# A Perceiver block on one core: VectorE and ScalarE in written order in the second cross-attention, and four longer step distances

## The chip, the cores and the metric

One Trainium2 chip, of which the kernel uses one core. The metric is the device time of one execution in microseconds (us), compared between runs of the kernel before and after the change on the same chip. PE is TensorE, PEld its weight loads, DVE VectorE, ACT ScalarE, POOL GpSimd, SP SyncE (it issues DMAs only).

## What is computed

Two layers over x of 16 x 64 rows of 256 numbers, all in float32. Each layer is a cross-attention to a context of 1024 rows per batch, a self-attention and a feed-forward part, each behind a layernorm and added to x. Cut to its shape:

```python
x = x + _L0_xattn_ref(_layernorm(x), ctx_1024, mask_BxS2_bf0, ...)      # 16 heads of 16
x = x + _L0_attn_ref(_layernorm(x), ...)                                # causal over the 16 batches
x = x + _L0_ffn_ref(_layernorm(x), ...)                                 # 8 experts, top 2
x = x + _L1_xattn_ref(_layernorm(x), ctx_1024, fside_BxS2_0, mask_BxS2_bk0, ...)
x = x + _L1_attn_ref(_layernorm(x), ...)                                # over the 64 rows of a batch
x = x + _L1_ffn_ref(_layernorm(x), ...)                                 # fp4 quantization, gate * up, down

def _L1_xattn_ref(tgt, mem, attn_bias, memory_key_padding_mask, ...):
    q = (tgt @ Wq_w.T + Wq_b).reshape(b, sq, 16, 16)
    kv = (mem @ Wkv_w.T + Wkv_b).reshape(b, sk, 2, 16, 16)
    scores = einsum('bthd,bshd->bhts', q, k * scale) + attn_bias + pad
    return einsum('bhts,bshd->bthd', softmax(scores), v).reshape(b, sq, 256) @ out_w.T + out_b
```

## The kernel before

**Rows and slots.** The 1024 rows lie in eight tiles x[0] to x[7] of 128 rows, so two batches share a tile. A cross-attention walks over 64 slots (batch, half of the heads, half of the keys), b the slowest and the key half the fastest. Four pairs of heads (g = 0 to 3) are worked on at a time; an odd slot holds the second half of the keys of the same heads.

**A slot.** In pass i of the loop, `scores` runs two slots ahead: four score matmuls (L567), each into a bank of PSUM, and four VectorE reductions (L578) that add the mask, write the tile e and keep a minimum. Where slot i + 2 holds a second half, four exponentials on ScalarE (L589) follow, one per e of 128 x 1024. Then slot i itself is turned: four groups k of four transposes (L597), each group into one bank, copied into eT by `evacuate` (L226 on VectorE, L228 on ScalarE; VectorE takes the first two groups of odd slots). At the end of the pass `attend` multiplies slot i - 1 with the values (L611). PSUM has eight banks; the attention's sum `pso` has one, everything else takes turns on the other seven.

**Keys and values.** The second cross-attention finds those of the first nine batches ready in DRAM, made during the first layer's later parts. Those of the other seven are projected in place, two steps per slot (L394 and L409), in slots 32 to 59; their results are evacuated by VectorE in odd slots and by ScalarE in even ones.

**Chains.** Everything that belongs to finished rows is written as generators that run beside the slots. `advance()` resumes every chain once, oldest first, after each group of transposes, so four times per slot; a `yield` is one step of distance, and `bare(n)` is n of them. `end(b)` starts at the end of slot 4b + 4 with `outputs`: copy of the sum (`ot`), reciprocal of the sums (`rec`, L628), turning (L633), scaling (`osb`, L636), and for the second batch of a tile a second turning (L649), `oT`, and the output projection `project_rows` (L322). In the second layer the same chain goes on with `row_attention` (layernorm L258 to L275, projections L1373, rotation L1393, scores L1428, exponential L1446, turning L1452, output L1468 and L1479, projection) and `feed_forward` (layernorm, quantization `fp4` in three steps, two halves of `hidden` L1520 with Silu L1523 and the product L1524, `fp4` of each half, `turn_hidden` L1530, `down` L1545). `queries` makes the queries of the next tile: it adds the two expert outputs that were gathered (`arrive`, L1279), normalizes, turns and projects. One tile takes eight slots, and a chain is longer than that, so that a tile's feed-forward runs beside the next tile's attention.

**What sets the order.** A planner (the tile framework) orders the instructions of each engine at build time, by priority (earlier in the program first) and by when its own timing model takes the inputs as ready. Inside `manual_schedule` the named engines are kept in the order in which the program is written. Before the change this holds for TensorE alone:

```python
            with tc.manual_schedule(engines={mybir.EngineType.PE}):
```

VectorE, ScalarE, GpSimd and the DMA queues are ordered by the planner in both cross-attentions. On the chip each engine runs the order that it was given.

Of the kernel before, what the change touches and what calls it, by code (L numbers as in the profile page):

```python
# [13 lines left out]
AF = mybir.ActivationFunctionType  # L14
# [106 lines left out]
def kernel(ctx: ExitStack, tc: tile.TileContext, a: dict, out: bass.AP):  # L121
    nc = tc.nc
# [127 lines left out]
    def bare(n):  # L250

        for _ in range(n):
            yield
# [77 lines left out]
    def cross_attention(layer, wq, wkv, wo, bq, bk, bv, bo, mask, keep, bias, after, ready, arrive, idle):  # L331
        side = "right" if layer else "left"
        with ExitStack() as st:
# [216 lines left out]
            slots = [(b, dt, hf) for b in range(B) for dt in range(KC) for hf in range(2)]  # L550
            mn, sums, es, eT, po, osb = {}, {}, {}, {}, {}, {}
            NG = 4

            def scores(b, dt, hf):


                if dt == 0 and hf == 0:
                    mn[b] = two.tile([P, 2, NP], F32, name="mn")
                    sums[b] = two.tile([P, NP], F32, name="sums")
                if hf == 0:  # L560
                    for g in range(NG):
                        es[b, dt, g] = wide.tile([P, SK], F32, name="e")
                cols = slice(hf * 512, (hf + 1) * 512)
                sc = [bank() for _ in range(NG)]
                for g in range(NG):
                    r = 32 * g
                    nc.tensor.matmul(  # L567
                        sc[g],
                        qm[b // 2][r : r + 32, dt, b % 2, :, :].rearrange("p j q -> p (j q)"),
                        kT[b][r : r + 32, dt, cols],  # L570
                        start=True,
                        stop=True,
                    )
                for g in range(NG):
                    pr = dt * NG + g
                    e = es[b, dt, g]

                    nc.vector.tensor_tensor_reduce(  # L578
                        out=e[:, cols],
                        in0=sc[g],  # L580
                        in1=negb[b][:, cols],
                        scale=1.0,
                        scalar=3e38 if hf == 0 else mn[b][:, 0, pr : pr + 1],
                        op0=ALU.add,
                        op1=ALU.min,
                        accum_out=mn[b][:, hf, pr : pr + 1],
                    )
                    if hf == 1:
                        nc.scalar.activation(  # L589
                            e, e, AF.Exp, scale=-1.0, bias=mn[b][:, 1, pr : pr + 1], accum_out=sums[b][:, pr : pr + 1]  # L590
                        )

            def transpose_keys(b, dt, k, vector):

# [24 lines left out]
            def outputs(b):  # L619


                n, half = b // 2, b % 2
                ot = two.tile([P, KC, P], F32, name="ot")
                evacuate(ot, po.pop(b), False)
                yield
                yield
                rec = two.tile([P, NP], F32, name="rec")
                nc.vector.reciprocal(rec, sums[b])  # L628
                if half == 0:
                    osb[n] = two.tile([P, NP, 2, HD], F32, name="osb")  # L630
                pq = bank()
                for c in range(KC):
                    nc.tensor.transpose(pq[:, c * P : (c + 1) * P], ot[:, c, :], ident)  # L633
                pov = pq[:, :D].rearrange("p (r j d) -> p r j d", j=2, d=HD)
                for j in range(2):
                    nc.vector.tensor_tensor(  # L636
                        osb[n][half * SQ : (half + 1) * SQ, :, j, :],
                        pov[j * SQ : (j + 1) * SQ, :, j, :],
                        rec[j * SQ : (j + 1) * SQ, :].unsqueeze(2).to_broadcast([SQ, NP, HD]),
                        ALU.mult,  # L640
                    )
                if half == 0:
                    return
                yield
                yield
                pt = bank()
                rows = osb[n].rearrange("p r j d -> p (r j d)")
                for c in range(KC):
                    nc.tensor.transpose(pt[:, c * P : (c + 1) * P], rows[:, c * P : (c + 1) * P], ident)  # L649
                oT = two.tile([P, KC, P], F32, name="oT")  # L650
                for c in range(KC):

                    nc.vector.tensor_scalar(
                        oT[:, c, :], pt[:, c * P : (c + 1) * P], colbias(bv, c), None, ALU.add
                    )
                yield
                yield
                project_rows(n, oT, wo, None if layer else rowbias(bo))
# [20 lines left out]
            def advance():  # L679
                for o in list(chains):  # L680
                    if next(o, o) is o:
                        chains.remove(o)
# [14 lines left out]
            else:  # L697
                load_keys(0)
                load_mask(0)
            with tc.manual_schedule(engines={mybir.EngineType.PE}):  # L700
                arrive(0, two, 0)
                chains.append(queries(0))
                if 0 not in ready:
                    project(0, 0)
                    advance()
                    project(0, 1)
                while chains:
                    advance()
                if not layer:
                    for w, source in soon[:2]:  # L710
                        nc.sync.dma_start(w, source)
                    load(1)
                    for w, source in soon[2:]:
                        nc.sync.dma_start(w, source)
                scores(*slots[0])
                scores(*slots[1])
                if 0 not in ready:
                    for step in range(2, NP):
                        project(0, step)
                for i in range(len(slots) + 1):  # L720

                    vector = i % 2 == 1
                    if i + 2 < len(slots):
                        scores(*slots[i + 2])
                    steps = due.pop(i, [])
                    for part in range(2):
                        for step in [s for s in steps if len(s) == 2][part::2]:
                            project(*step, vector)
                        for step in [s for s in steps if len(s) == 3]:
                            project_seven(*step, part)  # L730
                        if i < len(slots):
                            b, dt, hf = slots[i]
                            for k in (4 * hf + 2 * part, 4 * hf + 2 * part + 1):
                                transpose_keys(b, dt, k, vector and part == 0)
                                advance()
                    if i > 0:
                        b, dt, hf = slots[i - 1]
                        for k in range(4 * hf, 4 * hf + 4):
                            attend(b, dt, k)
                        if dt == KC - 1 and hf == 1:  # L740
                            chains.append(end(b))
                            next(chains[-1])
                    if i % 4 == 0 and i // 4 + 2 < B:
                        load(i // 4 + 2)
                        if seven:
                            sum_context(i // 4 + 2)
                        if i == 4:
                            for w, source in later:
                                nc.sync.dma_start(w, source)
                            later.clear()  # L750
                    if not layer and i == 4 * (B - 1) - 1:
                        for first in load_first:
                            load_ahead(first)
                    if i % 8 == 0 and i // 8 + 1 < NT:
                        arrive(i // 8 + 1, two, 0)
                    if i % 8 == 2 and i // 8 + 1 < NT:
                        chains.append(queries(i // 8 + 1))
                        next(chains[-1])
                while chains:
                    advance()  # L760
                    advance()
                    idle(1)
# [587 lines left out]
    def last_layers(one):  # L1350
# [11 lines left out]
        def row_attention(n, two):  # L1362
# [2 lines left out]
            nc.gpsimd.tensor_tensor(x[n], x[n], rowbias("L1_attn_b_proj"), ALU.add)  # L1365
            yield from bare(4)
            xT = transposed_rows(two, xn)
            yield
            yield
            pm = bank()  # L1370
            for i, (w, dt) in enumerate((w, dt) for w in (wq, wk) for dt in range(KC)):
                for c in range(KC):
# [76 lines left out]
            for dt in range(KC):  # L1449
# [5 lines left out]
                        ident,  # L1455
                    )
                evacuate(eT[:, dt, :, :], pt.rearrange("p (g q) -> p g q", g=NG), False)
            yield
            yield


            po = [bank() for _ in range(2)]
# [38 lines left out]
        def feed_forward(n, two):  # L1501
# [63 lines left out]
            else:  # L1565
# [6 lines left out]
                turn_hidden(0)  # L1572
                yield
                yield from fp4(tiles, h[:, halves[1]], h[:, halves[1]], P, NI - 3 * P, 3 * P)
                yield from bare(2)
                turn_hidden(3)
                yield from bare(3)
                py = bank()[:, :D]
# [109 lines left out]
```

## Time and profile before

| | |
|---|---|
| time, median of 3 runs (lowest to highest) | 1532.1 us (1530.3 to 1533.7) |
| the profiled execution's own time | 1533.16 us |
| its span, first to last instruction | 1531.1 us |
| first layer and what lies before the second cross-attention | 0 to 868 us |
| slots of the second cross-attention | 868 to 1440 us |
| rest of the last two chains | 1440 to 1531 us |
| turns of eight slots without projections in place (slots 9-16, 17-24, 25-32) | 58.9, 74.6, 77.9 us |
| turns with them (33-40, 41-48, 49-56) | 86.5, 85.5, 85.4 us |
| exponentials L589 | 256 x 1139 ns |
| score reductions L578 | 512, of 685 ns (first key half) and 747 ns (second) |
| eT copies | 384 x 587 ns on ScalarE, 128 x 682 ns on VectorE |

A slot is taken here from the start of one group of score matmuls to the start of the next, and numbered by its pass i of the loop. The profile lists for each engine how long it was busy, and for a wait the instruction that ended it. A wait on one of the seven banks shows as a wait on the instruction that emptied the bank, a VectorE reduction or a copy, and not on a producer of data.

### The profile page before, as it was taken

The numbers are of one execution on the slowest core, as the hardware profiler recorded it, in microseconds if no ns is written. First come the engines' busy times: TensorE is split into PE (matmuls) and PEld (weight loads), VectorE is DVE, ScalarE is ACT, GpSimd is POOL, SyncE is SP. The second block draws the span as 40 slices with busy tenths as digits, with TensorE's granted clock in tenths as the row PEclk, the third lists the DMA queues.
The fourth block names the chain that finished last, engine by engine and source line by source line (L and its number), as shares of the span: only waits on it lengthen the run. The fifth ranks groups of instructions, "written<-read, shape, count | busy, mean of one in ns | idle before, by whom it ended". The sixth has DMA issues, their size and how long they took to land.

```text
span 1531.1 us, 33572 instructions
## 1 busy us (share of the span) xinstructions
PE 1393.2 (91%) x13796; PEld 997.1 (65%) x13796; DVE 953.7 (62%) x2573; ACT 759.2 (50%) x1385; POOL 336.2 (22%) x368
## 2 busy tenths in 40 slices
PE   6999999999999898999999789787889999999954
PEld 3677667776776655668888566565656767666732
DVE  3577767777777432365730277786867586767654
ACT  2565666565656531223221476665645555555620
POOL 4344443343332120013300022120201011110000
PEclk9999999999999999999999799898999999999977
DMA  6111101110101022277773332322101111000000
GB/s 231 59 36 40 52 32 33 37 58 33 32 29 56 37 96 71 92 262 230 253 277 120 125 125 98 128 80 77 52 22 35 49 53 49 22 26 1 5 1 7
DMA packets 53556, 119.53 MB, mean 78 GB/s; under 512 B 4908, under 2 KB 25004, under 8 KB 51100
## 3 DMA queue, kind: packets, MB, share of 16 engines
q1 hardware_dynamic: 50732, 112.21, 21.8%
q0 software_dynamic: 1568, 4.26, 1.0%
q8 instruction: 108, 1.77, 0.5%
q10 hardware_dynamic: 1104, 0.93, 0.2%
q14 instruction: 44, 0.36, 0.1%
HBM read 94.32 MB, written 23.07 MB: 77 GB/s over the span
## 4 chain that ended last, share of the span: by engine, by line
PE 72%; DVE 16%; ACT 6%; issue 3%; DMA 2%; POOL 1%; ACTq 0%; DVEq 0%; SPq 0%; POOLq 0%
PE psw L597 11%; PE psw L567 9%; PE pso L611 8%; PE psw L458 6%; PE psw L462 5%; DVE e L578 5%; ACT e L589 4%; PE psw L1227 4%; PE psw L796 4%; PE psw L1247 4%; PE psw L409 3%; PE psw L394 3%; PE psw L783 3%; PE psw L1520 2%; PE psw L1545 2%
## 5 line engine op out<-in xcount | busy, mean ns | idle before, releaser
L589 ACT ACTIVATE e<-e,mn 128x1024 f32<-128x1024 f32 x256 | 291.1, 1139 | 114.5 <-DVE mn L578 113.7
L597 PEld LDWEIGHTS psw<-consts,e 128*128 128x128 f32 x2048 | 240.5, 144 | 104.1 <-issue 62.4
L597 PE MATMUL psw<-consts,e 128*128 128x128 f32 x2048 | 287.3, 280 | 8.3 <-ACT e L589 4.3
L228 ACT COPY eT<-psw 128x512 f32<-128x512 f32 x384 | 209.3, 587 | 156.2 <-PE psw L597 156.2
L578 DVE CUSTOM_DVE_ANT_0 e<-psw,negb,mn 128x512 f32<-128x512 f32 x256 | 179.6, 747 | 138.6 <-PE psw L567 138.6
L578 DVE CUSTOM_DVE_ANT_0 e<-psw,negb 128x512 f32<-128x512 f32 x256 | 163.0, 685 | 67.4 <-PE psw L567 67.4
L567 PE MATMUL psw<-kT,qm 32*128 32x512 f32 x1024 | 170.4, 682 | 8.5 <-DVE mn L578 4.4
L611 PE MATMUL pso<-eT,v 128*32 128x128 f32 x4096 | 146.9, 287 | 0.0
L611 PEld LDWEIGHTS pso<-eT,v 128*32 128x32 f32 x4096 | 110.2, 114 | 27.7 <-issue 26.2
L226 DVE COPY eT<-psw 128x512 f32<-128x512 f32 x128 | 83.0, 682 | 7.5 <-PE psw L597 7.5
L567 PEld LDWEIGHTS psw<-kT,qm 32*128 32x128 f32 x1024 | 52.9, 195 | 42.5 <-issue 22.8
L796 PE MATMUL psw<-w_L_xattn_Wkv_w,actx 128*128 128x256 f32 x288 | 74.2, 411 | 2.2 <-issue 1.4
L359 POOL TENSOR_SCALAR negb<-m 128x1024 f32<-128x1024 uint8 x16 | 16.7, 1045 | 264.4 <-DVE mn L578 214.7
L783 PE MATMUL psw<-actx,w_L_xattn_Wkv_w 128*128 128x512 f32 x144 | 67.4, 608 | 1.3 <-DVE x L769 1.3
L796 PEld LDWEIGHTS psw<-w_L_xattn_Wkv_w,actx 128*128 128x128 f32 x288 | 58.4, 207 | 15.3 <-issue 5.0
L790 ACT ACTIVATE astage<-psw,colb 128x512 f32<-128x512 f32 x36 | 24.6, 687 | 80.8 <-PE psw L783 47.3
L462 PEld LDWEIGHTS psw<-wgT,actx 128*128 128x128 f32 x448 | 53.3, 192 | 10.6 <-ACT eT L228 5.3
L462 PE MATMUL psw<-wgT,actx 128*128 128x128 f32 x448 | 58.3, 278 | 0.0
L1227 PE MATMUL psw<-xeT,w 128*128 128x256 f32 x256 | 56.6, 380 | 0.8 <-issue 0.8
L1247 PE MATMUL psw<-w,hT 128*128 128x256 f32 x256 | 56.6, 379 | 0.0
L458 PE MATMUL psw<-actx,wgT 128*128 128x512 f32 x112 | 56.4, 605 | 0.0
L409 PE MATMUL psw<-w_L_xattn_Wkv_w,ctxT 128*128 128x256 f32 x224 | 55.6, 392 | 0.0
(282 smaller groups left out, 2255.9 us busy)
## 6 DMA issues: line engine op xcount, KB each, us to landing
ctxT<-in_ctxT_dram SPq DMA_DIRECT2D x23, 1024.0 KB, 5.0
w<-in_L_ffn_w_dram SPq DMA_DIRECT2D x16, 1024.0 KB, 6.5
actx<-in_ctxT_dram SPq DMA_DIRECT2D x9, 1024.0 KB, 5.5
kd<-astage SPq DMA_DIRECT2D x36, 256.0 KB, 4.0
vd<-astage SPq DMA_DIRECT2D x36, 256.0 KB, 2.5
kT<-kd SPq DMA_DIRECT2D x9, 1024.0 KB, 6.2
v<-vd SPq DMA_DIRECT2D x9, 1024.0 KB, 4.8
ab<-in_fside_BxS_dram SPq DMA_DIRECT2D x32, 256.0 KB, 3.5
```

What stands on the lines that cost most here:

```text
L228: nc.scalar.copy(dst, src)
L458: nc.tensor.matmul(pm, a_, x_, start=True, stop=True)
L462: nc.tensor.matmul(pm[:, cols], x_[:, cols], a_, start=True, stop=True)
L567: nc.tensor.matmul(sc[g], qm[b // 2][r : r + 32, dt, b % 2, :, :].rearrange("p j q -> p (j q)"), kT[b][r : r + 32, dt, cols], start=True, ...
L578: nc.vector.tensor_tensor_reduce(out=e[:, cols], in0=sc[g], in1=negb[b][:, cols], scale=1.0, scalar=3e38 if hf == 0 else mn[b][:, 0, pr : ...
L589: nc.scalar.activation(e, e, AF.Exp, scale=-1.0, bias=mn[b][:, 1, pr : pr + 1], accum_out=sums[b][:, pr : pr + 1])
L597: nc.tensor.transpose(pt[:, g * P : (g + 1) * P], es[b, dt, g][:, k * P : (k + 1) * P], ident)
L611: nc.tensor.matmul(po[b][32 * g : 32 * g + 32, dt, :], v[b][:, k, pr * 32 : (pr + 1) * 32], e[:, g, :], start=(k == 0), stop=(k == NK - 1),)
L783: nc.tensor.matmul(pm, w1kv[:, c, dt * P : (dt + 1) * P], actx[b][:, c, cols], start=(c == 0), stop=(c == KC - 1),)
L796: nc.tensor.matmul(pm[:, j * D : (j + 1) * D], actx[b][:, c, (k + j) * P : (k + j + 1) * P], w1kv[:, c, D : 2 * D], start=(c == 0), stop=( ...
L1227: nc.tensor.matmul(ph[:, j * CAP : (j + 1) * CAP], w1[:, c, (f + j) * P : (f + j + 1) * P], xeT[:, c, :], start=(c == 0), stop=(c == KC - 1),)
L1247: nc.tensor.matmul(py[:, j * D : (j + 1) * D], hT[:, f, j * P : (j + 1) * P], w2[:, f, :], start=(f == 0), stop=(f == FF // P - 1),)
```

## The change

Three things are edited.

- In the second cross-attention (`layer` is 1) VectorE and ScalarE join TensorE in `manual_schedule`: all three issue in the order in which the program is written. In the first one TensorE alone is kept so.
- The exponentials leave `scores`. It returns a list of them, and the second layer's loop writes the first one right behind the reductions and one more behind each group of transposes, ahead of the chains' step there. The first layer's loop writes all four right behind `scores`.
- Four distances grow by one step: from `osb` to its turning (second layer alone), from the turned rows to the projections in `row_attention`, from the turned weights to the output there, and from the second half's quantization to `turn_hidden(3)` in `feed_forward`. All later steps of a chain move with them.

```diff
@@ scores, inside the loop over g
-                    if hf == 1:
-                        nc.scalar.activation(
-                            e, e, AF.Exp, scale=-1.0, bias=mn[b][:, 1, pr : pr + 1], accum_out=sums[b][:, pr : pr + 1]
-                        )
+                return [] if hf == 0 else [(b, dt * NG + g, es[b, dt, g]) for g in range(NG)]
+
+            def exponentials(b, pr, e):
+                nc.scalar.activation(
+                    e, e, AF.Exp, scale=-1.0, bias=mn[b][:, 1, pr : pr + 1], accum_out=sums[b][:, pr : pr + 1]
+                )
@@ outputs, between osb and its turning
-                yield
-                yield
+                yield from bare(3 if layer else 2)
@@ cross_attention
-            with tc.manual_schedule(engines={mybir.EngineType.PE}):
+
+            engines = {mybir.EngineType.PE}
+            if layer:
+                engines |= {mybir.EngineType.DVE, mybir.EngineType.Activation}
+            with tc.manual_schedule(engines=engines):
...
-                scores(*slots[0])
-                scores(*slots[1])
+                for i in range(2):
+                    for each in scores(*slots[i]):
+                        exponentials(*each)
...
-                    if i + 2 < len(slots):
-                        scores(*slots[i + 2])
+                    exps = scores(*slots[i + 2]) if i + 2 < len(slots) else []
+                    if exps:
+                        exponentials(*exps.pop(0))
+                    if not layer:
+                        while exps:
+                            exponentials(*exps.pop(0))
...
                                 transpose_keys(b, dt, k, vector and part == 0)
+                                if exps:
+                                    exponentials(*exps.pop(0))
                                 advance()
@@ row_attention, between transposed_rows and the projections
-            yield
-            yield
+            yield from bare(3)
@@ row_attention, between the turned weights and the output
-            yield
-            yield
+            yield from bare(3)
@@ feed_forward, between fp4 of the second half and turn_hidden(3)
-                yield from bare(2)
+                yield from bare(3)
```

## The prediction

> **What bounds the kernel now.** I read the page first, then TensorE's waits, then the stretches slot by slot, then the timeline of single slots. The page gives the busy shares and, in 40 slices, where they are lost (rows: TensorE, VectorE, granted clock).
>
> ```profile
> PE 1393.2 (91%) x13796; PEld 997.1 (65%) x13796; DVE 953.7 (62%) x2573; ACT 759.2 (50%) x1385; POOL 336.2 (22%) x368
> ...
> PE   6999999999999898999999789787889999999954
> ...
> DVE  3577767777777432365730277786867586767654
> ...
> PEclk9999999999999999999999799898999999999977
> ```
>
> TensorE is the bound. Slices 23 to 37 (880 to 1440 us) are the second cross-attention, the only stretch that the diff reorders; there TensorE falls to 7 and 8 tenths and VectorE climbs to 8. The waits of TensorE from 895 to 1445 us (total us, times, longest) name the places:
>
> ```profile
> PE psw L649 <- DVE osb L636: 24.3, 7, 4.5
> PE psw L1468 <- ACT turned L228: 10.9, 3, 3.6
> PE psw L1530 <- DVE mn L578: 3.8, 2, 1.9
> PE psw L1428 <- ACT qm L537: 3.7, 2, 1.9
> PE psw L597 <- DVE mn L578: 3.1, 6, 1.3
> ```
>
> The first three, 39.0 us, are the steps whose distance the diff lengthens. Stretches cut at the starts of the score matmuls (L567) give slots; here slots 41 and 42 and the sum over 41 to 48, one turn of eight slots (columns: length, busy PE, PEld, DVE, ACT, POOL, granted clock):
>
> ```profile
> 1221.70:1233.80 12.10, 8.48 (x76) 4.93 (x72) 11.70 (x34) 5.96 (x11) 3.55 (x3) 0.97 0.18 56
> 1233.80:1246.20 12.40, 12.40 (x93) 8.69 (x90) 7.61 (x29) 6.20 (x10) 0.72 (x1) 0.89 0.01 2
> ...
> sum 85.40, PE 81.53 PEld 56.53 DVE 61.82 ACT 48.25 POOL 12.71; mean PE 10.19 PEld 7.07 DVE 7.73 ACT 6.03 POOL 1.59
> ```
>
> Slot 41 is VectorE's (11.70 of 12.10 us), every other slot of this turn is TensorE's. The turn 982.7 to 1057.3, before the in-place projections begin at slot 32, takes 74.6 us with PE 61.83 and DVE 56.30: nobody is full, they take turns. The timeline shows how VectorE's order sets that:
>
> ```profile
> 1231.69 0.29 DVE L636 TENSOR_TENSOR osb<-psw,rec 64x128 f32<-64x128 f32 x1
> ...
> 1232.04 0.44 PE L649 MATMUL psw<-consts,osb 128*128 128x128 f32 x2 [3.62 <-DVE osb L636]
> ...
> 1247.42 0.75 DVE L578 CUSTOM_DVE_ANT_0 e<-psw,negb,mn 128x512 f32<-128x512 f32 x1 [0.30 <-PE psw L567]
> 1248.10 0.42 DVE L258 BATCH_NORM_STATS2 bnst<-x 128x6 f32<-128x256 f32 x1
> 1248.43 0.73 DVE L578 CUSTOM_DVE_ANT_0 e<-psw,negb,mn 128x512 f32<-128x512 f32 x1
> ```
>
> In slot 41 osb comes after a feed-forward layernorm and its first quantization, and TensorE waits 3.62 us. In slot 43 the planner does the opposite: the score reductions (L578) go ahead of the layernorm of the next rows, which is written before them and is threaded between them.
>
> **The change, part by part.** One chain of rows takes four steps per slot, step 0 at the end of a slot 8m. The four added yields move L649 from step 4 to 5, the row attention's layernorm from 7 to 8, the feed-forward's from 32 (end of slot 8m+8) to 35 (third step of slot 8m+9), hidden halves from 40 and 44 to 43 and 47.
>
> *Removed.* The 39.0 us above, if nothing takes their place: L649 lands behind an attend (1.0), scores (1.1), four transposes (0.5) and, where slots project, one projection (1.9).
>
> *VectorE in slots 8m+1 and 8m+2.* I lay the written order out for a projecting turn, from slot 41's scores at 0. Durations from the trace: four reductions 2.7 us (2.45 for the first halves), an eT copy 0.65, a kT evacuation 0.73, rec and osb 0.8, x add 0.45, first quantization step 1.6, second 1.05, third 0.9, oT 0.67, gathered adds 1.0. A layernorm that stands alone takes 3.24 us, from the first of these rows to the end of the second:
>
> ```profile
> 1499.51 0.43 DVE L258 BATCH_NORM_STATS2 bnst<-x 128x6 f32<-128x256 f32 x1
> ...
> 1502.33 0.41 DVE L275 TENSOR_SCALAR xnr<-x,mvr,rsd 128x256 f32<-128x256 f32 x1
> ```
>
> Slot 41: reductions end at 3.9, the evacuation and two copies 5.9, x add 6.3, osb 7.1 (before: 1231.98 - 1221.7 = 10.3), second evacuation 7.8, feed-forward layernorm 11.1, quantization 12.7. TensorE, unhindered, ends the slot at 9.2, so L649 at 12.7 finds osb done: its wait is gone. But the reductions of slot 42's scores now start at 12.7 and not at 10.4. TensorE has seven banks (eight less one); the allocation seven back must be free. Counting along: 0.3 us lost on the reductions, 0.6 on oT (16.9). Then VectorE has x add (18.3), layernorm (21.6), adds (22.6), layernorm of the queries (25.9), a block of 7.5 us in front of slot 43's reductions. TensorE starts those scores at 19.4, passes one projection, one transpose group and one small transpose (23.3), and its next bank needs the first reduction, 26.6: 3.3 us, and 0.2 on the second. Sum 4.4 us against 3.62 removed. Slot 43 would then end at 34.2, as before (34.3), but with 1.2 us less of chain work behind it (6.2 against 7.4 us, since hidden half two has gone to slot 44). **+1.1 us a turn; slots 33 to 59 are 3.4 turns: +4.**
>
> *The same without projections.* TensorE has only 5.5 us of work in each of slots 17 and 18. VectorE's run from 1.2 to 24.4 us is unbroken, and TensorE waits 3.3, 3.0 and 4.7 us inside it. Carried on through slots 19 to 24 (waits of 0.8, 1.3 and 1.9 more, one half-clock stretch on the path) I get 75 us against 74.6: here 4.5 (L649), 3.6 (L1468), 1.9 (L1530) and 1.9 (L1428) go, and about as much comes. **Two turns: +1.** Slots 9 to 16, with no feed-forward yet, come to 57 against 58.9: **-2.** Slots 1 to 8, attention alone, 10.3 us a pair by the same count against 10.6: **-1.**
>
> *Exponentials.* The fourth is now queued behind the copy of the third transpose group, and ScalarE cannot start it before. Projecting, that group is turned at 7.7, the exponential (1.14) ends at 9.4 and is first read at 12.2: hidden with 2.8 us to spare. In a bare slot it ends at 7.1 where TensorE could read it at 6.9; 0.2 us a pair is in the 10.3. If cover is gone everywhere it costs 1.14 in each of 32 pairs.
>
> *Table loads.* Both Silu halves now stand with no exponential between them (after the fourth of slot 8m+3, and in slot 8m+4, which has none): one pair of 1.28 us loads less per block. ScalarE is 48.25 of 85.40 busy: nothing on the path. A new wait on VectorE does stand there: h (L1524) waits for Silu behind three exponentials, 2.6 us idle in slot 43, with one quantization step and slot 44's reductions behind it; TensorE's next bank is free by then, so I take 0, and 1.0 a turn if not.
>
> *The clock.* Half rate comes in stretches of 3.41 us, sixteen of them from 895 to 1440: at most 16 x 3.41 / 2 = 27 us.
>
> ```profile
> 1011.10:1014.50 3.40, 1.50 (x13) 1.00 0.00 0
> 1014.50:1017.90 3.40, 3.40 (x19) 0.51 0.02 5
> ```
>
> 1.50 us busy of 3.40 (0.44) is enough to halve the next stretch; stretches of 0.50 and more did not. The moved waits (3.3, 3.0, 4.7) leave less than that, so I keep the sixteen: 0, from -27 to +10 (six more).
> The Trainium skill (TensorE: Matmul & The Clock Gate, "What's actually happening") says that the clock halves after at least one idle window of about 3.4 us; by that, a stretch 44% busy would have stayed at full rate, and waits of 3.3 us would cost no clock, which would make the sum some 15 us lower. The trace differs, and I go by the trace.
>
> *First layer and tail.* The first layer's exponentials are written later but on an engine where nothing lies between: 0, at most +-1. The tail (91.5 us from 1439.6) is one dependency chain beside a second; four steps more, same work: 0, bounds -3 and +4.
>
> Sum: +4 +1 -2 -1 = **+2**. The profiled execution is 1533.2 (span 1531.1 and 2.1 around it); 1535.2, less 1.1, by which the median of the runs (1532.1) lies below it: **1534**. What this kernel's measurement can tell from no change is about 0.2%, 3 us.
>
> **The rivals.**
> *Faster: the distances act and the blocks are passed.* If banks come free in another order than I counted, or the queue before was already close to the written one, only the distances work: L649 keeps the 1.8 us that its bank needs and gives 7 x 1.8 = 12.6, L1468 10.9, L1530 3.8: -27, so 1505; with all 39.0, 1493. For it: reductions and exponentials already run in written order in most slots. Against: slot 43's rows above, where they don't.
> *Slower: VectorE's blocks come in full.* The place is the layernorm pair ahead of the reductions of slots 8m+3. It decides from the point where VectorE enters that block more than 1.5 us later than I have it (fp4 steps slowed beside GpSimd took 1.21 instead of 0.18 us at 1228.9). Then a turn loses 6.7 us and two half stretches (3.4) for the 5.3 removed: +4.8 x 3.4 = +16, and 1548. For it: strict order cannot use VectorE's 3.3 us of idleness ahead of 1220.35. Against: osb and kT now come earlier.
>
> **How the numbers follow.** The sum near zero: 0.45, own range 1526 to 1543; of it 0.12 is faster by over 0.2%, 0.17 within, 0.16 slower. Distances alone or more: 0.26. Blocks in full: 0.29. Faster 0.38, same 0.17, slower 0.45. The range goes down to 1504 (the distances alone, without its further half) and up to 1552 (blocks and tail, 1548 + 4), leaving out about 0.2.
>
> **What would show it.** Right: L649's wait gone; TensorE's waits on mn (L578) up from 3 us to 20 or more, at the third or second transpose group of slots 8m+2 and 8m+3; L258 to L275 unbroken; Silu and Exp loads 14 and 13 down to about 8 each; turns of 86.5 us. Wrong: mn waits below 10 us (faster), or turns over 89 us and more than 20 half stretches (slower).

## The result and the profile after

| | before | after |
|---|---|---|
| median (lowest to highest) | 1532.9 us (1530.3 to 1534.8) | 1557.2 us (1556.2 to 1557.7) |
| ratio, 95% interval | | 1.0159 (1.0141 to 1.0176) |
| span of the profiled execution | 1531.1 us | 1555.4 us |

The change makes the kernel 24 us slower: the largest of the three chances, but a time beyond the range. In the changed kernel exponentials are L591, transposes L599, the second turning that was L649 is L650, oT L654, the product h L1534.

The page (busy times; then 40 slices of the span in tenths):

```profile
PE 1406.5 (90%) x13796; PEld 1007.9 (65%) x13796; DVE 972.8 (63%) x2573; ACT 746.1 (48%) x1373; POOL 336.3 (22%) x368
...
PE   6999999999999898899999798697989989899855
...
DVE  4577777776777342564711567877777666867664
...
PEclk9999999999999998989999798888899999999977
```

PE has the same 13796 instructions, busy 13 us longer, in part because more of them ran at half rate (PEclk is 8 tenths in slices 25 to 29; before, in two of these five). ScalarE has 12 instructions fewer: from 880 to 1470 us there are six table loads each for Silu and for Exp, where there were 13 and 12. TensorE's waits from 895 to 1445 us (total, times, longest):

```profile
PE psw L599 <- DVE mn L578: 35.9, 14, 5.0
PE psw L322 <- DVE oT L654: 4.1, 2, 2.1
PE psw L567 <- issue: 3.7, 2, 1.8
PE psw L1530 <- ACT xTr L292: 3.6, 2, 2.0
...
PE psw L1439 <- DVE mn L578: 1.7, 9, 0.2
```

The wait of L650 on osb is gone, and the transposes' wait for a bank that a score reduction still reads (mn) has taken its place. Slots 41, 43 and 46 and the turn's sum (length, busy PE, PEld, DVE, ACT, POOL, granted clock):

```profile
1230.66:1239.31 8.65, 8.65 (x82) 5.28 (x74) 7.16 (x20) 5.19 (x9) 3.55 (x3) 1.00 0.13 40
...
1249.47:1266.96 17.49, 13.62 (x88) 9.90 (x84) 12.13 (x39) 8.02 (x14) 3.71 (x4) 0.80 0.24 76
...
1289.37:1301.96 12.59, 11.77 (x111) 9.21 (x107) 8.65 (x25) 4.84 (x12) 0.94 (x2) 0.86 0.01 2
...
sum 91.61, PE 86.00 PEld 60.14 DVE 63.68 ACT 46.38 POOL 12.85; mean PE 10.75 PEld 7.52 DVE 7.96 ACT 5.80 POOL 1.61
```

Slot 41 has lost its 3.6 us, slot 43 is the worst of the turn. Its timeline (start, duration, engine, line; in brackets the idle time and who ended it):

```profile
1248.13 0.42 DVE L324 TENSOR_TENSOR x<-psw,x 128x256 f32<-128x256 f32 x1 [0.18 <-PE psw L322]
...
1248.59 0.43 DVE L258 BATCH_NORM_STATS2 bnst<-x 128x6 f32<-128x256 f32 x1
...
1249.47 1.14 PE L567 MATMUL psw<-kT,qm 32*128 32x512 f32 x8
...
1251.40 0.41 DVE L275 TENSOR_SCALAR xnr<-x,mvr,rsd 128x256 f32<-128x256 f32 x1
1251.73 1.35 DVE L1291 SCALAR_TENSOR_TENSOR x<-g,rt_w,x 128x256 f32<-128x256 f32 x2
...
1255.93 0.41 DVE L275 TENSOR_SCALAR xnq<-x,mvr,rsd 128x256 f32<-128x256 f32 x1
1256.25 0.74 DVE L578 CUSTOM_DVE_ANT_0 e<-psw,negb,mn 128x512 f32<-128x512 f32 x1
...
1257.06 1.11 PE L599 MATMUL psw<-consts,e 128*128 128x128 f32 x4 [3.87 <-DVE mn L578]
```

The scores are multiplied from 1249.47; their first reduction starts at 1256.25, behind two whole layernorms; TensorE waits 3.87 us. What the wait then costs, in three stretches of 3.4 us (length, PE, ..., clock):

```profile
1252.80:1256.20 3.40, 0.39 (x4) 0.15 (x2) 2.98 (x14) 0.00 (x0) 2.09 (x2) 1.00 0.19 48
1256.20:1259.60 3.40, 2.54 (x8) 2.26 (x9) 3.40 (x11) 2.56 (x6) 0.72 (x1) 0.50 0.08 29
1259.60:1263.00 3.40, 3.40 (x11) 2.55 (x10) 1.91 (x4) 1.68 (x4) 0.00 (x0) 0.50 0.18 17
```

One stretch 12% busy, and the next two run at half rate. TensorE is busy in them for 2.54 and 3.40 us; at full rate that work would take half the time at the least, so they cost at most 3.0 us on top of the wait of 3.9.

### The profile page after: what moved, and what is told of

The parts are those of the page before. It is cut to its first block, busy times and chain, and to the rows that moved or that the text cites. A ratio compares the mean times of both kernels' runs of the same rounds, so it can differ in the third digit from the quotient of the medians.

```text
span 1555.4 us, 33604 instructions
## 1 busy us (share of the span) xinstructions
PE 1406.5 (90%) x13796; PEld 1007.9 (65%) x13796; DVE 972.8 (63%) x2573; ACT 746.1 (48%) x1373; POOL 336.3 (22%) x368
## 5 line engine op out<-in xcount | busy, mean ns | idle before, releaser
L591 ACT ACTIVATE e<-e,mn 128x1024 f32<-128x1024 f32 x256 | 292.1, 1142 | 144.0 <-DVE mn L578 143.2
L599 PE MATMUL psw<-consts,e 128*128 128x128 f32 x2048 | 296.8, 284 | 46.5 <-DVE mn L578 36.8
L599 PEld LDWEIGHTS psw<-consts,e 128*128 128x128 f32 x2048 | 245.9, 146 | 143.1 <-issue 55.4
L567 PE MATMUL psw<-kT,qm 32*128 32x512 f32 x1024 | 165.8, 660 | 9.3 <-issue 3.7
L613 PE MATMUL pso<-eT,v 128*32 128x128 f32 x4096 | 143.4, 283 | 0.0
L409 PE MATMUL psw<-w_L_xattn_Wkv_w,ctxT 128*128 128x256 f32 x224 | 62.2, 426 | 1.4 <-DVE osb L638 1.4
L409 PEld LDWEIGHTS psw<-w_L_xattn_Wkv_w,ctxT 128*128 128x128 f32 x224 | 44.4, 208 | 20.3 <-issue 4.0
```

Of the source, the lines that this page charges most:

```text
L409: nc.tensor.matmul(pm[:, j * D : (j + 1) * D], ctxT[b][:, c, (k + j) * P : (k + j + 1) * P], wkv[:, c, D : 2 * D], start=(c == 0), stop=(c ...
L567: nc.tensor.matmul(sc[g], qm[b // 2][r : r + 32, dt, b % 2, :, :].rearrange("p j q -> p (j q)"), kT[b][r : r + 32, dt, cols], start=True, ...
L591: nc.scalar.activation(e, e, AF.Exp, scale=-1.0, bias=mn[b][:, 1, pr : pr + 1], accum_out=sums[b][:, pr : pr + 1])
L599: nc.tensor.transpose(pt[:, g * P : (g + 1) * P], es[b, dt, g][:, k * P : (k + 1) * P], ident)
L613: nc.tensor.matmul(po[b][32 * g : 32 * g + 32, dt, :], v[b][:, k, pr * 32 : (pr + 1) * 32], e[:, g, :], start=(k == 0), stop=(k == NK - 1),)
```

## The experiments

Each is a short edit of the kernel before or after. Ratios are to the kernel before, with 95% intervals. The turns are sums of slot lengths, cut as in the prediction.

**1. The parts apart.** Distances alone: the four added yields on the kernel before.

> The four longer distances alone; order of VectorE and ScalarE left to the planner, exponentials where they were. Theory A (the written order of VectorE costs the time: a block of layernorm, adds and layernorm stands in front of the reductions of slots 8m+3): with the planner's order the block goes, the waits on osb, turned and h shrink, 1505 to 1520 us. Theory B (the longer chains themselves cost, since more chain work overlaps): 1540 us or more. Theory C (ScalarE's order and the place of the exponentials cost): as theory A here.

1512.1 us, 0.9888 (0.9853 to 0.9924). Turn 41 to 48 takes 82.1 us (before 85.5, after 91.5). The order alone, with the old distances:

> VectorE and ScalarE in written order with the exponentials behind the transposes, but the distances of before. Theory A: the block is in the same place, and the waits on osb come back on top: 1560 to 1570 us. Theory B: the chains are as short as before, so most of the 24 us goes: 1530 to 1540 us. Theory C: 1555 us.

1537.9 us, 1.0041 (1.0026 to 1.0057). So the distances save 19 us, the order costs 6 by itself, and both together cost 24 instead of saving 13. Theory A's 1560 to 1570 us is missed here: the waits on osb are back (28.1 us), but VectorE reaches the layernorms of slots 42 and 43 with idle time ahead of them, slot 43's reductions start 3.8 us behind their scores (6.8 in the changed kernel), and the slot takes 10.8 us. In these two traces whole layernorms in written order cost much only where VectorE comes to them late. Then one engine at a time:

```diff
-                engines |= {mybir.EngineType.DVE, mybir.EngineType.Activation}
+                engines |= {mybir.EngineType.DVE}           # vector only
+                engines |= {mybir.EngineType.Activation}    # scalar only
```

> All of the change, but only TensorE and VectorE in written order, ScalarE by the planner. Theory A: 1552 to 1560 us, nearly the changed kernel's 1557. Theory C: near the distances alone, 1505 to 1525 us.

> All of the change, but only TensorE and ScalarE in written order, VectorE by the planner. Theory A: near the distances alone, 1505 to 1525 us. Theory C: 1550 us or more.

VectorE alone in written order: 1550.8 us, 1.0126 (1.0101 to 1.0150). ScalarE alone: 1513.7 us, 0.9878 (0.9851 to 0.9905), the distances alone again. Nearly the whole loss is VectorE's order. The place of the exponentials is nothing: all four behind the reductions, in written order,

> The changed kernel, but all four exponentials written right behind the score reductions, as before the change, on a ScalarE in written order. If the place of the exponentials (one behind each transpose) costs or saves nothing, as counted: 1553-1561. If the late fourth exponential holds TensorE: 1540-1550. If it keeps the evacuations of ScalarE from standing behind four exponentials: 1564 or more.

gave 1556.5 us, 1.0168 (1.0133 to 1.0203).

**2. What the planner does in slot 43.** Timeline of VectorE in the distances alone (scores multiplied from 1223.51):

```profile
1224.75 0.16 DVE L274 SCALAR_TENSOR_TENSOR rsd<-nwt,rsd 128x1 f32<-128x1 f32 x1
1224.82 0.74 DVE L578 CUSTOM_DVE_ANT_0 e<-psw,negb,mn 128x512 f32<-128x512 f32 x1
...
1225.49 0.27 DVE L273 TENSOR_SCALAR nwt<-rsd,var 128x1 f32<-128x1 f32 x1
1225.68 0.74 DVE L578 CUSTOM_DVE_ANT_0 e<-psw,negb,mn 128x512 f32<-128x512 f32 x1
...
1226.35 0.15 DVE L274 SCALAR_TENSOR_TENSOR rsd<-nwt,rsd 128x1 f32<-128x1 f32 x1
1226.42 0.74 DVE L578 CUSTOM_DVE_ANT_0 e<-psw,negb,mn 128x512 f32<-128x512 f32 x1
...
1227.09 0.41 DVE L275 TENSOR_SCALAR xnr<-x,mvr,rsd 128x256 f32<-128x256 f32 x1
```

The reductions start 1.3 us after their scores (6.8 in the changed kernel), and the layernorm's small dependent steps lie between them. Two readings follow: the reductions must go first, or the layernorms must not stand whole.

**3. Who goes first: four tries.** The adds and layernorm of the queries four steps later, with four bare steps fewer behind them:

> The changed kernel with the gathered adds and the layernorm of the queries (4.2 us of VectorE) written four steps later, at the end of slot 8m+3 and so ahead of the reductions of slot 8m+4; the queries are turned at the same step as before. Theory A (the block in front of the reductions of slots 8m+3 is what costs): slot 43 falls from 17.5 to 11 or 12 us, six such slots, 1522 to 1535 us. Theory A2 (VectorE's run of slots 8m+1 to 8m+3 as a whole, wherever its last layernorm stands): the wait moves to slot 44, 1545 to 1557 us.

1548.1 us, 1.0126 (1.0081 to 1.0170). Slot 43 falls to 10.5 us, slot 44 rises from 11.9 to 15.3. There the turning of the rows waits for the end of the same layernorm (xnq, at 1259.89) and then for a bank:

```profile
1259.48 0.41 DVE L275 TENSOR_SCALAR xnq<-x,mvr,rsd 128x256 f32<-128x256 f32 x1
...
1260.56 0.44 PE L290 MATMUL psw<-consts,xnq 128*128 128x128 f32 x2 [3.18 <-DVE mn L580]
```

The feed-forward's layernorm back at step 32, with L650's distance kept:

> Written order with the distance of osb kept at three, but row attention one step shorter than before the change (both its longer distances undone, and the pair of steps ahead of its projection made one), so that the feed-forward's layernorm and first quantization stand at steps 32 and 33 again, in and just behind the light slot 8m+8. The block in front of slot 8m+3's reductions stays. Theory A (block and the 4.9 us of backlog in front of it together): TensorE passes the block, slot 43 at 11 to 13 us, 1528 to 1540 us. If the block alone decides: 1550 us or more.

1554.7 us, 1.0162 (1.0131 to 1.0192): slots 42 and 43 take 15.8 and 16.0 us. The last chain step of slots 8m+2 and the queries' start behind the reductions of slot 8m+3, in these slots and then in three of every four (the short diff is of the first):

```diff
+                                if layer and i % 8 == 2 and k % 4 == 3:
+                                    tardy.append(advance)      # called after the next scores()
+                                else:
                                     advance()
```

> In slots 8m+2 the last chain step (the x add and the row attention's layernorm) and the start of the next rows' queries (gathered adds, their layernorm) are written behind slot 8m+3's score reductions instead of ahead of them; nothing else is changed. Theory A (the loss is that the block of two layernorms stands ahead of the reductions): slot 43 falls from 17.5 to 10.5-12.5 us, the waits of TensorE on mn in these slots vanish, some half-rate stretches with them, 1520-1540. Theory B (VectorE in a written order has no give, whatever stands first): the evacuations and the copies behind the block are late instead, slots 43 and 44 together stay above 27 us (29.4 in the changed kernel) and the time stays 1548 or more.

> As the one before, but in every slot of the second cross-attention, except each fourth one, the last chain step is written behind the next slot's score reductions (the queries' start too). Theory A: slot 46's loss (12.6 against 9.05 us with the planner's order) goes as well, and slots 17 to 32 come back by some us: 1512-1530, at most near the distances alone (1512). Theory B: no better than the one before, 1548 or more. In between, 1530-1548, the place of the reductions is part of it and something else the rest.

1555.5 us, 1.0152 (1.0115 to 1.0188), and 1560.3 us, 1.0182 (1.0142 to 1.0222). "Reductions first" falls as a remedy for the whole: the first of the two wins 8.0 us over the changed kernel in slots 33 to 60 (300.7 against 308.7) and loses 6.3 in slots 1 to 16. TensorE's waits in it:

```profile
PE psw L599 <- DVE mn L578: 10.8, 6, 3.7
PE psw L567 <- DVE eT L226: 10.4, 4, 3.7
PE psw L599 <- DVE v L226: 10.1, 3, 3.4
```

The wait on mn fell from 35.9 to 10.8 us, and 20.5 came back as waits on evacuations (v, eT), which in slot 43 stand behind the same two layernorms.

**4. The layernorms in pieces.** VectorE in written order as in the changed kernel, but row attention's and the queries' layernorm yield twice inside; two bare steps go behind each, so that their readers keep their places:

```diff
             for i in range(3):
+                if pieces and i != 1:
+                    yield
                 nc.vector.tensor_scalar(t, r, va, r, ALU.mult, ALU.mult)
```

> The changed kernel, VectorE in written order, with two of its layernorms (row attention's and the next rows' queries') cut in three pieces of about 1.5, 0.9 and 0.9 us, a chain step apart; the bare steps behind them are two fewer, so that what reads them keeps its place. Theory C (the whole layernorms, 3.24 us that nothing is threaded into, are what the written order costs): the block ahead of slot 43's reductions falls from 7.5 to 4.8 us, TensorE's 3.9 us there to about 1 and the half-rate stretch with it: slot 43 at 11-14 us instead of 17.5, slots 41 to 48 at 83-86, 1530-1543. Theory B (any block that is moved or cut is paid for elsewhere, since VectorE's written order as a whole leaves no slack there): slot 43 better, its gain back in slots 44 and 45, 1548-1558.

1524.3 us, 0.9949 (0.9931 to 0.9966): 33 us less than the changed kernel, more than was expected. Slot 43 and the turn's sum, and VectorE in front of slot 43's reductions (L580 there):

```profile
1230.60:1241.70 11.10, 10.82 (x90) 7.76 (x86) 10.51 (x37) 7.80 (x14) 3.05 (x4) 1.00 0.39 120
...
sum 84.00, PE 81.98 PEld 56.98 DVE 63.22 ACT 45.98 POOL 12.80; mean PE 10.25 PEld 7.12 DVE 7.90 ACT 5.75 POOL 1.60
```

```profile
1229.22 0.42 DVE L326 TENSOR_TENSOR x<-psw,x 128x256 f32<-128x256 f32 x1 [0.18 <-PE psw L324]
...
1230.81 0.14 DVE L271 TENSOR_SCALAR var<-var 128x1 f32<-128x1 f32 x1
1230.87 1.00 DVE L1293 SCALAR_TENSOR_TENSOR x<-g,rt_w,x 128x256 f32<-128x256 f32 x2
...
1233.03 0.14 DVE L271 TENSOR_SCALAR var<-var 128x1 f32<-128x1 f32 x1
1233.09 0.74 DVE L580 CUSTOM_DVE_ANT_0 e<-psw,negb,mn 128x512 f32<-128x512 f32 x1
```

VectorE's work in the turn is the same (63.2 against 63.7 us), but the block is 3.9 us instead of 8.1, the wait and its half-rate stretches are gone (slot clock 1.00). All three layernorms in pieces, and the queries two steps later:

> As the one before, the queries' adds and layernorm two steps later besides, and the feed-forward's layernorm in three pieces too (two bare steps fewer behind its quantization). Theory C: slots 41 to 48 at 80-84 us, slots 17 to 32 back by some us, 1518-1535. Theory B: 1545 or more.

1520.1 us, 0.9922 (0.9899 to 0.9945). Both runs stay behind the distances alone (1512.1 us); what holds them there was not shown. Pieces together with the reductions first:

> The reductions of slots 8m+3 first (as in the run of 1555 us) and the two layernorms in pieces. Theory C: what held that run up (3.35 us for a projection's evacuation behind the two whole layernorms) goes, since only 4.8 us and not 7.7 stand ahead of it: 1525-1540. Theory B: 1548 or more.

1550.7 us, 1.0115 (1.0092 to 1.0139), against the expectation. Its first wait is

```profile
PE psw L292 <- DVE xnr L277: 22.2, 6, 8.2
```

The pieces begin behind the reductions and end two steps later, while the turning of the rows, which reads them, keeps its step. The control, the two layernorms in pieces under the planner's order with the longer distances:

> The distances alone, VectorE and ScalarE in the planner's order, with the same two layernorms cut in the same pieces: the control to the run of 1524 us. Theory C (the cut gives the written order what the planner does by itself): nothing to be had here, 1507-1518. If the cut helps by itself, whoever orders VectorE (33 us in written order): 1490 or less.

1517.1 us, 0.9907 (0.9891 to 0.9924), 5 us more than without, where the two intervals overlap. The cut is worth 33 us in written order and nothing in the planner's: it does by hand what the planner does (section 2).

**5. Clock and tail.** Six spare matmuls of 128x256 in slots 8m+3 of the changed kernel, into a bank's free half:

> The changed kernel with six matmuls of 128x256 (about 3.1 us) more in each slot 8m+3 from slot 11 on, behind the first transpose group, where TensorE waits 3.9 us; they write a spare half of the attention's bank that nobody reads. If the half-rate stretches after that wait cost time (clock theory): the wait is filled, the two stretches behind it go, about 3.4 us for each of seven slots: 1535 to 1548 us. If the clock is no part of it: 1557 us, or more where the matmuls outlast the wait.

1553.4 us, 1.0138 (1.0114 to 1.0161): 3.8 us less, between the two expectations, far short of the 9 to 22 us that the clock theory asked for. Time at half rate in slots 1 to 60 falls from 88.4 to 61.0 us. Turns 33 to 40 and 41 to 48 lose 6.8 us of it each and 3.4 and 2.7 us of time, as two half stretches are worth. By slots: 35 and 38 lose one stretch and 1.7 us each, 43 two stretches and 2.6 us, 51 one stretch and 1.3 us; slot 54 gains one and 1.7 us, so that turn 49 to 56 keeps its 3.4 us of half rate and wins nothing. Slots 25 to 32 lose 10.2 us of half rate and only 0.9 of time, and slots 57 to 60, with no stretch in either run, take 2.3 us more: there the spare work itself costs. So the clock is a part of the loss, worth 1.3 to 1.7 us a stretch where slots project; for the other slots its share was not isolated. The tail with VectorE in the planner's order:

> The changed kernel, but in the loop behind the last slot (the last two chains) only TensorE keeps its written order. The rest from slot 61 took 106.6 us after the change against 99.5 before. If VectorE's written order makes that (two layernorms one behind the other instead of threaded): 1550 to 1552 us. If the longer distances make it: 1557 us.

1557.7 us, 1.0173 (1.0150 to 1.0195): not VectorE's order in that loop. From slot 61 to the end the profiles have 99.5 us before, 102.4 with the distances alone, 106.6 after (105.6 in this run), 96.8 with the order and old distances, 97.5 with three steps taken out of the chain again: in written order a step costs the tail 2.5 to 3 us, in the planner's order 0.7. VectorE alone in written order has 107.6 us, ScalarE alone 102.7: the dearer step comes with VectorE's order in the slots ahead of that loop. Which wait makes it was not shown.

**6. Further distances.** Two more steps (behind oT and behind the turned rows) on the distances alone, and on the written order with pieces:

> The distances alone with the planner's order, and two more steps lengthened from two to three: a row's output projection behind oT (L322 waited 12.0 us on oT in the distances alone) and the hidden matmuls behind the turned rows (11.5 us). If the planner again fills what the distances open: 1490-1508. If one step more only pushes the chains of the last rows into the tail: 1510-1520.

> VectorE in written order with all three layernorms in pieces and the queries two steps later (1520 us), with the two further distances that took the planner's version from 1512 to 1507. If they act here too: 1508-1516, still behind the planner's 1507. If the written order turns them into later blocks: 1518-1530.

1506.6 us, 0.9842 (0.9804 to 0.9879), and 1507.0 us, 0.9846 (0.9821 to 0.9871): the fastest versions, 25 us below the kernel before and 50 below the change, one in each order.

## Why the prediction was wrong

| term | predicted | measured (profiles) | of it half rate, at most |
|---|---|---|---|
| slots 33 to 60 | +4 | +12.3 | 3.5 |
| slots 17 to 32 | +1 | +6.2 | 4.0 |
| slots 9 to 16 | -2 | +0.3 | 0.7 |
| slots 1 to 8 | -1 | +2.0 | 3.1 |
| half-rate stretches, slots 1 to 60 | 16 kept, 0 | 54.8 to 88.4 us, 26 | 11.3 |
| up to slot 1 | 0 | -3.5 | |
| tail | 0 (-3 to +4) | +7.1 | |
| sum | +2 | +24.3 | |

The last column is half of the time that TensorE was busy inside half-rate stretches, after less before. It is an upper bound: a projection of 1.99 us took 3.62 at half rate, less than double.

**Held, almost to the digit.** The mechanism was right up to slot 43. L649's wait went; the table loads fell to half; the layernorms run unbroken. From slot 41's scores the reductions of slot 43 were to start at 25.9 us and TensorE to go on at 26.6 after a wait of 3.3; they start at 25.6, it goes on at 26.4 after 3.87. Silu's hold on VectorE was to be 2.6 us and is 3.8.

**The clock was kept at zero: the largest step that failed.** The prediction read a rule (a stretch less than half busy halves the next one, stretches of 0.50 and more did not), placed 3.3, 3.0 and 4.7 us of wait, and let them replace old stretches one for one. The rule left out what the trace of before already held: in four of the sixteen stretches the clock was halved behind another half stretch that was 60 to 100% busy. One of these pairs (length, busy PE, granted clock, DMA):

```profile
1140.80:1144.20 3.40, 1.19 (x9) 1.00 0.31 77
1144.20:1147.60 3.40, 2.00 (x30) 0.51 0.50 118
1147.60:1151.00 3.40, 3.40 (x22) 0.50 0.00 0
```

So one wait could bring two stretches. Besides, slots 41 to 43 were laid out with durations at full rate and set against 34.3 us of before that hold a half stretch. After the change slots 1 to 60 have 26 stretches where they had 16, at most 11.3 us. In the turn 41 to 48 there are three for one: slot 43 was to end at 34.2 and ends at 36.3, although TensorE goes on as counted at 26.4, with the two stretches (at most 3.0 us) in between. How much of the 11.3 us is on the path is shown only where stretches were removed (experiment 5, projecting turns).

**A projecting turn was mis-sized at full rate too.** Turns 33 to 40 and 49 to 56 have as many half stretches as before, two and one, and still take 4.2 and 3.0 us more, against +1.1. With the bound of the last column taken off, the three turns take 83.7 to 83.8 us before and 86.9 to 87.2 after: +3.1 to +3.5. Taken so, the turn 41 to 48 is 0.6 us longer up to the end of slot 43, and slots 44 to 48 take 2.4 us more where the count, which ended at slot 43, had allowed 1.2.

**Slot 46 was not laid out.** It takes 2.0 us more than before, with a half stretch (1.7) in it; without that it takes 10.9 us, in the planner's order 9.1. Of these 1.8 us, 1.3 are in the scores of the row attention: the same 32 matmuls take 2.4 us after and 1.1 in the distances alone, because two of them need banks that the score reductions (mn) free, which VectorE's written order has behind osb, an evacuation and a quantization step:

```profile
1293.80 0.56 PE L1439 MATMUL psw<-rkT,rqm 32*128 32x64 f32 x4
1294.54 0.43 PE L1439 MATMUL psw<-rkT,rqm 32*128 32x64 f32 x2 [0.18 <-DVE mn L578]
1295.15 1.10 PE L1439 MATMUL psw<-rkT,rqm 32*128 32x64 f32 x26 [0.18 <-DVE mn L578]
...
1261.12 1.12 PE L1426 MATMUL psw<-rkT,rqm 32*128 32x64 f32 x32
```

(The first three lines are the changed kernel, the last one the distances alone.) The half stretch follows one that the records show as 89% busy; its cause stays open.

**Turns 17 to 32** were carried on by hand from the same count; it missed them by 5 us, with 17.1 us more of half rate, which are at most 4.0 of the 6.2 us. Where the rest is was not shown.

**The tail** was "same work, 0". It takes 7.1 us more, beyond the bound of +4: 2.9 us come with the four longer distances in the planner's order, the rest with VectorE's written order (experiment 5).

**The rivals.** "Blocks in full" gave the sign and nearly the price (16 us for slots 33 to 60, measured 12.3), but its condition, VectorE entering the block 1.5 us later, is not what happened: it entered on time and the stretches came anyway, though two behind one block only in the turn 41 to 48. That the price is near is in part luck. "Distances alone" was right about the distances (1505 expected, 1512 measured) and wrong about who lets them act: the planner does, the written order of the same program does not. The 3.5 us before the first slot are of code that the second cross-attention's order does not touch; between profiles that stretch varies from 876 to 881 us.

**The clock rule.** The Trainium skill (TensorE: Matmul & The Clock Gate, "What's actually happening") asks for at least one idle window before the clock halves. The trace of after has two halved stretches behind one that was 12% busy, so the trace decides again, as it did in the prediction.

## What to carry to other kernels

A written order fixes the unit in which an engine changes hands: before giving an engine to it, look for the longest piece of program without a point of exchange (here two layernorms, 8.1 us with what lies between) and cut it, rather than argue who goes first; each way of putting others first only chose another victim. Longer distances and a written order are not additive; try each alone. Price a new wait of TensorE at its length plus the half-rate stretches that follow it (here up to 1.7 us each, and sometimes two), count a repeating pattern to its end, and price a step added to a chain at what it costs where the chain runs alone.

## What the runs showed of the hardware

One wait can be followed by two half-rate stretches of 3.41 us: after the change behind a wait of 3.9 us, the second behind a stretch that was 75% busy, and in the trace of before in four places. Where slots project, the spare matmuls took single stretches away and 1.3 to 1.7 us with each.

Not expected: a half-rate stretch came in slot 46 behind one in which the records show TensorE busy over 85% (1293.8 to 1297.2 us). It comes where the scores of the row attention take 2.4 us instead of 1.1, in some turns and not in others with the same order (slots 38 and 46 but not 54 after; 46 and 54 but not 38 with the spare matmuls); no run explains it.
